# Loading the first image in pieces ahead of the weights, the second ahead of the zero fills, and moving the second image's statistics

## The chip, the cores and the metric

The kernel runs on one core of a Trainium2 chip. The metric is the device time of one execution in microseconds (us); less is better. One core has TensorE (PE in the profile, its weight loads PEld), VectorE (DVE), ScalarE (ACT), GpSimd (POOL) and SyncE (SP), each with its own queue of instructions that it runs in order, and 16 DMA engines.

## The reference, cut to what matters

Four images of 56 x 56 positions and 128 channels pass through four layers. Each layer normalizes its input by groups of four channels over the whole image, applies a block and adds the result to its input.

```python
def _gn(v, G=32, eps=1e-5):
    B_, H_, W_, C_ = v.shape
    g = v.reshape(B_, H_, W_, G, C_ // G)
    m = jnp.mean(g, axis=(1, 2, 4), keepdims=True)
    s = jnp.var(g, axis=(1, 2, 4), keepdims=True)
    return ((g - m) / jnp.sqrt(s + eps)).reshape(v.shape)

x = x + L0(_gn(x))   # window attention 7x7, full attention over 3136 positions, MLP
x = x + L1(_gn(x))   # projection, 3x3 depthwise convolution, selective scan in four directions, gate
x = x + L2(_gn(x))   # deformable 3x3 convolution (gathers at computed places)
x = x + L3(_gn(x))   # as L0, with weights of its own
```

What matters here: the group norm of a layer needs the sums over a whole image before anything of that layer can begin, and the images are independent of each other.

## The kernel before, in words

An image lies in fast memory as 128 channels x 3136 positions of float32 (1568 KB). Two such buffers exist, `xs[0]` and `xs[1]`; image b uses `xs[b % 2]`. The work on an image is cut into seven pieces of 448 positions (`NCK` pieces of `CH`).

*Start.* `__init__` loads the packs of weights: "C" (constants) and "L1" on SyncE's queue, "L0" and "L3" on ScalarE's, by `load` (L115 in the profile). It sets small constants. Then `run` issues the load of image 0 as one transfer (L1521), calls `swin_prepare` for L0 and L3 (one small matmul each, L198, and an addition, L199, which need that layer's weights), `mamba_prepare` (an exponential on ScalarE, L759, and two small operations on VectorE, L760 and L762, on weights of L1) and `deform_prepare`. The latter fills four tables in main memory with zeros, one for each image, from one small tile of zeros: for each table a transfer of 3364 KB (L1297) and one of 1 KB (L1300), on SyncE's queue. Behind them `run` issues the load of image 1 (L1526).

*Statistics.* `stats(b, c)` (L123) is one `bn_stats` on VectorE over piece c of image b. `group_norm` puts the seven together (L143), takes group means with a matmul (`gn_pm`, L145), the variance with another (`gn_pv`, L152), and the root on ScalarE (L154).

*The loop over images.* For each image `run` emits the seven statistics and then layer L0's attention, its MLP together with L1's convolution, L1's scan and L1's output; L2 of an image is woven beside the next image's L0 and L1, and L3 follows. For images that come later the statistics follow the loading of each piece at the end of L3 of the image that had the buffer before (`finish`, L1504 and L1506).

*The order.* Most stages are written under a manual schedule, which keeps the order of the code. Outside of these, and between stages, a scheduler places instructions in each engine's queue. VectorE's statistics of image 1 are emitted at the head of the loop's second turn; nothing before them writes that buffer, and the scheduler has put them far ahead of their place in the code, into the window stage of image 0.

*The window stage* (`windows`, inside `attention`) works through bands of windows: tokens (L243), projections (L251), scores (L276), their maxima and subtraction (L282, L283), exponentials (L286), normalization (L290, L291, and L294 on GpSimd), transposes (L300), and the full attention's inputs for the piece that is ready (L423 to L431) and first row maxima (L368, L373). After it comes the main attention loop, whose first matmuls are L540 and L549.

*L1's output stage* (`mamba_out`) runs a pipeline over seven pieces: mean, subtraction (L1226) and squares (L1228), gate (L1240), root (L135, L136), scaling (L1252, L1254), gating (L1258), the output matmul (L1264), and `store`, which adds the result to x (L1267) and takes the piece's statistics for L2 (L123).

Of the kernel before, what the change touches and what calls it, by code (L numbers as in the profile page):

```python
# [10 lines left out]
F32 = mybir.dt.float32  # L11
# [8 lines left out]
P = 128  # L20
HW = 56
L = HW * HW
CH = 448
NCK = L // CH
# [54 lines left out]
class _Net:  # L79
    def __init__(self, ctx, tc, x, packs, out):  # L80
        self.tc, self.nc, self.x_in, self.out, self.packs = tc, tc.nc, x, out, packs
        self.B = x.shape[0]
        nc = self.nc
        wp = ctx.enter_context(tc.tile_pool(name="weights", bufs=1))
        self.keep = wp
        self.w = {}
        for i, layer in enumerate(("C", "L0", "L1", "L3")):
            self.load(layer, wp, nc.sync if i % 2 == 0 else nc.scalar)
        c = self.w["C"]
        self.ident, self.gmat = c["ident"], c["gmat"]  # L90
        self.ones = {1: c["ones1"], 2: c["ones2"]}
        self.center = {1: (c["center1"],), 2: (c["center2"], c["others2"])}
        self.sel = wp.tile([P, KB], F32R, tag="sel", name="sel")
        nc.vector.memset(self.sel.bitcast(F32), 0.0)
        for h in range(NH):
            nc.vector.memset(self.sel[h * DK : h * DK + 2, :].bitcast(F32), 1.0)
        self.ident2 = wp.tile([64 + NX, NX], F32R, tag="ident2", name="ident2")
        nc.vector.memset(self.ident2.bitcast(F32), 0.0)
        for k in (0, 64):
            nc.vector.tensor_copy(self.ident2[k : k + NX, :], self.ident[:NX, :NX])  # L100
        self.all1 = wp.tile([P, P], F32, tag="all1", name="all1")
        nc.vector.memset(self.all1, 1.0)
        self.one32 = self.all1[:, :DK]
        self.eps = wp.tile([P, 1], F32, tag="eps", name="eps")
        nc.vector.memset(self.eps, 1e-5)
        self.any = wp.tile([P, 1], F32, tag="any", name="any")
        self.xs = [wp.tile([P, L], F32, tag=f"x{i}", name=f"x{i}") for i in range(2)]
        self.sts = [wp.tile([P, NCK, 6], F32, tag=f"gn_st{i}", name=f"gn_st{i}") for i in range(2)]
        self.dpool = ctx.enter_context(tc.tile_pool(name="tables", bufs=1, space=DRAM))

# [1096 lines left out]
    def mamba_out(self, b, ya, gn):  # L1207


        nc, tc, w, x = self.nc, self.tc, self.w["L1"], self.x_of(b)  # L1210
        with tc.tile_pool(name="mo", bufs=2) as sb, tc.tile_pool(name="mo_ps", bufs=8, space=PSUM) as ps, tc.manual_schedule():
            bank = lambda name: ps.tile([P, 512], F32, tag="mm", name=name)
            part = lambda c: slice(c * CH, (c + 1) * CH)
            m = {}

            def mean(c):
                pm = m["pm", c] = bank("pm")
                for j in range(2):
                    nc.tensor.matmul(pm[:, :CH], lhsT=self.center[2][1], rhs=ya[:, j, part(c)], start=(j == 0), stop=(j == 1))

            def less(c):
                pm = m.pop(("pm", c))
                xc = m["xc", c] = sb.tile([P, 2, CH], F32, tag="xc", name="xc", bufs=4)
                sq = m["sq", c] = sb.tile([P, 2, CH], F32, tag="sq", name="sq")
                for j in range(2):
                    nc.vector.tensor_add(xc[:, j, :], pm[:, :CH], ya[:, j, part(c)])  # L1226
                for j in range(2):
                    nc.scalar.activation(sq[:, j, :], xc[:, j, :], AF.Square)  # L1228

            def tokens(c):  # L1230
                m["xg", c] = sb.tile([P, CH], F32, tag="xg", name="xg2")
                self.gn_apply(m["xg", c], x[:, part(c)], gn)

            def gate(c):
                xg = m.pop(("xg", c))
                z = m["z", c] = sb.tile([P, 2, CH], F32, tag="z", name="z", bufs=3)
                for j in range(2):
                    pz = bank("pz")
                    nc.tensor.matmul(pz[:, :CH], lhsT=w["w_in"][:, (2 + j) * P : (3 + j) * P], rhs=xg, start=True, stop=True)
                    nc.scalar.activation(z[:, j, :], pz[:, :CH], AF.Silu)  # L1240

            def spread(c):
                sq, pv = m.pop(("sq", c)), bank("ln_pv")
                for j in range(2):
                    nc.tensor.matmul(pv[:, :CH], lhsT=self.all1, rhs=sq[:, j, :], start=(j == 0), stop=(j == 1))
                rs = m["rs", c] = sb.tile([P, CH], F32, tag="rs", name="rs")
                self.table_of_both()
                self.one_over_root(rs, pv[:, :CH], 0.5 / P)

            def scale(c):  # L1250
                xc, rs = m["xc", c], m.pop(("rs", c))
                nc.vector.tensor_mul(xc, xc, rs[:, None, :].to_broadcast([P, 2, CH]))  # L1252
                for j in range(2):
                    nc.scalar.activation(xc[:, j, :], xc[:, j, :], AF.Identity, bias=w["ln_b"][:, j : j + 1], scale=w["ln_w"][:, j : j + 1])  # L1254

            def gated(c):
                xc = m["xc", c]
                nc.vector.tensor_mul(xc, xc, m.pop(("z", c)))  # L1258

            def out(c):  # L1260
                xc = m.pop(("xc", c))
                po = m["po", c] = bank("pmo")
                for j in range(2):
                    nc.tensor.matmul(po[:, :CH], lhsT=w["w_out"][:, j * P : (j + 1) * P], rhs=xc[:, j, :], start=(j == 0), stop=(j == 1))  # L1264

            def store(c):
                nc.vector.tensor_add(x[:, part(c)], x[:, part(c)], m.pop(("po", c))[:, :CH])  # L1267
                self.stats(b, c)

            def do(f, c):  # L1270
                if 0 <= c < NCK:
                    f(c)

            tokens(0)
            for c in range(-1, NCK + 1):
                do(mean, c + 1)
                do(gated, c - 1)
                do(less, c + 1)
                do(scale, c)
                do(gate, c + 1)  # L1280
                do(out, c - 1)
                do(tokens, c + 2)
                do(spread, c + 1)
                do(store, c - 1)
# [233 lines left out]
            self.weave(self.mlp("L3", b, x1, oT, True, side is None), side)  # L1518

    def run(self):  # L1520
        self.nc.sync.dma_start(self.xs[0], self.x_in[0])  # L1521
        self.swin_prepare("L0")
        self.swin_prepare("L3")
        self.mamba_prepare()
        self.deform_prepare()
        self.nc.sync.dma_start(self.xs[1], self.x_in[1])  # L1526
        for b in range(self.B):
            for c in range(NCK):
                self.stats(b, c)
            with ExitStack() as mb:  # L1530
                s1, made = ExitStack(), {}
                made["at"] = self.swin_attention("L0", b, s1)
                self.weave(self.first_half(b, s1, mb, made, b == 0), self.deform(b - 1) if b > 0 else None)
                self.mamba(b, made["pool"], made)
            if b > 0:
                self.last_layer(b - 1, self.deform(b) if b == self.B - 1 else None)
        self.last_layer(self.B - 1)
# [91 lines left out]
```

## Time and profile before

| | us |
|---|---|
| median of 3 runs | 12171.69 |
| lowest and highest | 12166.93, 12178.63 |
| the profiled execution | 12171.84 |
| its span in the profile | 12169.8 |

| engine | busy us | share of the span |
|---|---|---|
| PE | 10926.0 | 90% |
| DVE | 9400.2 | 77% |
| POOL | 9398.7 | 77% |
| ACT | 7551.3 | 62% |

The granted clock of TensorE had a mean of 0.956 of full speed. Lines of the timeline read: start in us, duration in us, engine, line of the kernel, operation, output and inputs, count, and in brackets the idle time before it and what ended that. "SPq" is SyncE's queue issuing a transfer. Lines of the waits read: who waited, for whom, then us in total, times, and the longest.

### The profile page before, as it was taken

The numbers are of one execution on the slowest core, as the hardware profiler recorded it, in microseconds if no ns is written. First come the engines' busy times: TensorE is split into PE (matmuls) and PEld (weight loads), VectorE is DVE, ScalarE is ACT, GpSimd is POOL, SyncE is SP. The second block draws the span as 40 slices with busy tenths as digits, with TensorE's granted clock in tenths as the row PEclk, the third lists the DMA queues.
The fourth block names the chain that finished last, engine by engine and source line by source line (L and its number), as shares of the span: only waits on it lengthen the run. The fifth ranks groups of instructions, "written<-read, shape, count | busy, mean of one in ns | idle before, by whom it ended". The sixth has DMA issues, their size and how long they took to land.

```text
span 12169.8 us, 219808 instructions
## 1 busy us (share of the span) xinstructions
PE 10926.0 (90%) x86844; PEld 7148.8 (59%) x86844; DVE 9400.2 (77%) x12051; ACT 7551.3 (62%) x19326; POOL 9398.7 (77%) x5876
## 2 busy tenths in 40 slices
PE   5998998998799989999879988999988998997799
PEld 3546886553588845454368875545446886553454
DVE  4758997775999967477699986747679998775674
ACT  3667776564577656656467775665646776564366
POOL 1976997596799939669679985957957997596497
PEclk8999999998899999999989999999988999998899
DMA  1000000004300000000420000000051000004200
GB/s 65 2 1 17 5 5 2 1 1 124 97 6 5 3 1 1 12 1 2 142 79 5 5 3 1 2 12 1 1 169 53 6 5 2 1 1 137 73 2 6
DMA packets 145431, 321.09 MB, mean 26 GB/s; under 512 B 17885, under 2 KB 86673, under 8 KB 144145
## 3 DMA queue, kind: packets, MB, share of 16 engines
q0 software_dynamic: 70848, 231.27, 6.5%
q1 hardware_dynamic: 73264, 74.17, 1.9%
q8 instruction: 686, 11.24, 0.4%
q14 instruction: 345, 2.82, 0.1%
q10 hardware_dynamic: 288, 1.59, 0.0%
HBM read 259.05 MB, written 47.90 MB: 25 GB/s over the span
## 4 chain that ended last, share of the span: by engine, by line
PE 59%; DVE 16%; POOL 11%; ACT 8%; issue 4%; SPq 1%; DMA 1%; DVEq 0%; POOLq 0%; ACTq 0%
PE pm L368 15%; PE po L576 10%; DVE hs L1123 10%; POOL hs L1132 8%; PE pst L549 7%; PE pst L540 3%; PE pd L565 2%; PE yt L1141 2%; PE pyb L1162 2%; PE pvt L1455 2%; PE dbu L1105 2%; PE pdo L1463 1%; DVE dgb L1009 1%; DVE mx L373 1%; PE pc L819 1%
## 5 line engine op out<-in xcount | busy, mean ns | idle before, releaser
L373 DVE TENSOR_REDUCE mx<-pm 128x1 f32<-128x512 f32 (+7 forms) x6424 | 3377.7, 560 | 996.7 <-PE pm L368 920.0
L560 POOL TENSOR_TENSOR es<-es,e 128x896 f32<-128x896 f32 x1824 | 3764.5, 2090 | 78.5 <-ACT e L550 30.7
L1123 DVE TENSOR_TENSOR_SCAN hs<-da,dbu 128x928 f32<-128x928 f32 x1792 | 3617.5, 2068 | 33.7 <-ACT dbu L1116 17.4
L550 ACT ACTIVATE e<-pst 128x448 f32<-128x448 f32 (+1 forms) x5600 | 2592.6, 549 | 1534.7 <-PE pst L549 1123.4
L1132 POOL TENSOR_TENSOR hs<-hs,cb 128x896 f32<-128x896 f32 x1792 | 3434.5, 1948 | 18.9 <-ACT carry L1127 16.7
L368 PE MATMUL pm<-ks,qs 32*128 32x448 f32 (+5 forms) x12848 | 2966.3, 529 | 103.6 <-DVE mx L373 90.3
L549 PE MATMUL pst<-qs,ks 32*128 32x448 f32 x11200 | 2326.0, 540 | 0.0
L368 PEld LDWEIGHTS pm<-ks,qs 32*128 32x128 f32 x12848 | 1282.7, 187 | 1209.7 <-DVE mx L373 712.3
L1141 PE MATMUL yt<-w_C,hs 128*116 128x128 f32 x14336 | 1877.7, 274 | 15.0 <-POOL hs L1132 13.3
L540 PE MATMUL pst<-nm,sel 32*128 32x448 f32 x5600 | 1667.7, 527 | 6.9 <-DVE nm L394 6.9
L1141 PEld LDWEIGHTS yt<-w_C,hs 128*116 128x116 f32 x14336 | 1569.4, 135 | 39.3 <-POOL hs L1132 29.3
L1105 PE MATMUL dbu<-dgb,ut 112*128 112x224 f32 x7168 | 1249.4, 297 | 202.1 <-DVE hs L1123 199.7
L576 PE MATMUL po<-e,va 128*32 128x448 f32 (+1 forms) x11200 | 1360.1, 554 | 0.0
L1330 POOL DMA_INDIRECT g<-tab,idx x900 | 871.0, 968 | 507.2 <-issue 207.0
L549 PEld LDWEIGHTS pst<-qs,ks 32*128 32x128 f32 x11200 | 1255.8, 187 | 1.5
L1060 ACT ACTIVATE da<-dl,A 128x112 f32<-128x112 f32 x3584 | 1193.3, 382 | 0.1
L1105 PEld LDWEIGHTS dbu<-dgb,ut 112*128 112x128 f32 x7168 | 947.8, 192 | 322.2 <-DVE hs L1123 309.8
L540 PEld LDWEIGHTS pst<-nm,sel 32*128 32x128 f32 x5600 | 711.7, 185 | 165.9 <-issue 147.7
L294 POOL TENSOR_TENSOR pz<-s,m 64x784 f32<-64x784 f32 x128 | 191.8, 1499 | 776.9 <-DVE m L291 772.4
L1127 ACT COPY carry<-hs 128x32 f32<-128x32 f32 x1792 | 396.0, 221 | 550.6 <-DVE hs L1123 529.5
L576 PEld LDWEIGHTS po<-e,va 128*32 128x32 f32 (+1 forms) x11200 | 222.9, 108 | 826.0 <-issue 766.2
L1077 PE MATMUL pt<-w_C,dh 128*112 128x128 f32 x3584 | 552.5, 278 | 154.1 <-DVE dgb L1009 148.0
(227 smaller groups left out, 14350.8 us busy)
## 6 DMA issues: line engine op xcount, KB each, us to landing
g<-tab,idx POOLq DMA_INDIRECT x900, 3.6
tab<-zero SPq DMA_DIRECT2D x4, 3364.0 KB
dl_d<-dl SPq DMA_DIRECT2D x28, 448.0 KB
dl<-dl_d SPq DMA_DIRECT2D x56, 224.0 KB
tab<-gt SPq DMA_DIRECT2D x16, 448.0 KB
out_dram<-x SPq DMA_DIRECT2D x28, 224.0 KB
tab<-gt SPq DMA_DIRECT2D x16, 336.0 KB
w_L<-in_L_dram SPq DMA_DIRECT2D x4, 973.0 KB
```

The costliest lines, as they stand in the source:

```text
L368: nc.tensor.matmul(pm[:, at : at + m], lhsT=qs[head(h), q : q + P], rhs=ks[head(h), keys], start=True, stop=True)
L373: nc.vector.tensor_reduce(mx[:, i, h, n : n + 1], p, AX.X, ALU.max)
L540: nc.tensor.matmul(pst[g, h][:, :CH], lhsT=self.sel[head(h), :], rhs=nm[head(h), part(g // NKB)], start=True, stop=False)
L549: nc.tensor.matmul(t[:, :CH], lhsT=ks[head(h), k * KB : (k + 1) * KB], rhs=qs[head(h), part(qc)], start=False, stop=True)
L550: nc.scalar.activation(es[g, p][:nk, j, :], t[:nk, :CH], AF.Exp, scale=SCALE)
L560: nc.gpsimd.tensor_tensor(s, es[g - 1, p][:nk] if k == 1 else s, es[g, p][:nk], ALU.add)
L576: nc.tensor.matmul(m["po"][head(h), :CH], lhsT=va[:nk, k, head(h)], rhs=src(h)[:nk], start=(k == 0), stop=(k == NKB - 1))
L1060: nc.scalar.activation(m["da"][:, :, n, 2:], dl(), AF.Exp, scale=A[:, j, n : n + 1])
L1105: nc.tensor.matmul(pu[:, 8 * h : 8 * h + 8, 2 + tb * TB : 2 + (tb + 1) * TB], lhsT=made[g]["ut", 2 * r + tb][:, d, :], rhs=made["r", g // ...
L1123: nc.vector.tensor_tensor_scan(flat(pairs[u // 2][:, d % 2]), flat(made[g]["da"][:, r]), flat(banks.pop(u)), 0.0, ALU.mult, ALU.add)
L1132: nc.gpsimd.tensor_tensor(hs, hs, made["r", g // 2]["cb"][:, :, r * HW : (r + 1) * HW], ALU.mult)
L1141: nc.tensor.matmul(sums[q][:YR, e * P : (e + 1) * P], lhsT=hs[:, n, :], rhs=self.ident, start=(n == 0), stop=(n == NST // 2 - 1), is_trans ...
```

## The change

Image 0 is loaded in seven pieces of 448 positions (224 KB each) at the very front of SyncE's queue; L0 and C are loaded on ScalarE's queue, L1 and L3 on SyncE's behind the pieces. Image 0's statistics are emitted before the preparations. Image 1 is loaded, still as one transfer, before the zero fills. Image 1's statistics are no longer emitted at the head of its turn but in `store` of L1's output stage of image 0, one piece after each of image 0's pieces.

```diff
         self.w = {}
-        for i, layer in enumerate(("C", "L0", "L1", "L3")):
-            self.load(layer, wp, nc.sync if i % 2 == 0 else nc.scalar)
+        self.xs = [wp.tile([P, L], F32, tag=f"x{i}", name=f"x{i}") for i in range(2)]
+        for c in range(NCK):
+            cols = slice(c * CH, (c + 1) * CH)
+            nc.sync.dma_start(self.xs[0][:, cols], x[0][:, cols])
+        for layer, queue in (("L0", nc.scalar), ("C", nc.scalar), ("L1", nc.sync), ("L3", nc.sync)):
+            self.load(layer, wp, queue)
...
-        self.xs = [wp.tile([P, L], F32, tag=f"x{i}", name=f"x{i}") for i in range(2)]
...
             def store(c):
                 nc.vector.tensor_add(x[:, part(c)], x[:, part(c)], m.pop(("po", c))[:, :CH])
                 self.stats(b, c)
+                if b == 0:
+                    self.stats(1, c)
...
     def run(self):
-        self.nc.sync.dma_start(self.xs[0], self.x_in[0])
+        for c in range(NCK):
+            self.stats(0, c)
         self.swin_prepare("L0")
         self.swin_prepare("L3")
         self.mamba_prepare()
+        self.nc.sync.dma_start(self.xs[1], self.x_in[1])
         self.deform_prepare()
-        self.nc.sync.dma_start(self.xs[1], self.x_in[1])
         for b in range(self.B):
-            for c in range(NCK):
-                self.stats(b, c)
+            if b > 1:
+                for c in range(NCK):
+                    self.stats(b, c)
```

In each engine's list of instructions the change shows as follows. SyncE's and ScalarE's loads stand in the new order. TensorE's and GpSimd's lists are the same as before. VectorE's list has image 0's statistics and their aggregation ahead of L1's and L3's preparations, has lost the seven statistics in the window stage of image 0, and has seven more in its L1 output stage, the last of them ahead of image 1's aggregation. ScalarE's list has one more table load at the start: the table of the root is loaded first, then that of the exponential for `A` (L759), then that of the root again before the root itself.

## The prediction

> **What bounds the kernel now.** The profiled execution took 12171.84 us for a span of 12169.8 us; the median of the runs is 12171.69 us, so a saving in the span can be taken off either. Over the whole span TensorE leads (PE 59% of the chain that ended last), and the change touches none of its work. I therefore read the waits of the first 260 us, the stretch that the diff rearranges.
>
> ```profile
> POOL pz L294 <- DVE m L291: 180.5, 8, 106.5
> ACT oTi L418 <- DVE ln_sq L415: 97.9, 5, 94.9
> DVE gn_st L123 <- DMA x<-in_x_dram: 95.9, 2, 92.8
> PE pm L368 <- DVE mx L373: 90.3, 1, 90.3
> ```
>
> Columns: total, times, longest. Every engine has one wait of 90 to 106 us, and all of them lead to VectorE (DVE), which itself waits 92.8 us for a load of x. The timeline of DVE shows which one; the last two lines are the same steps for the second image.
>
> ```profile
> 71.07 0.56 DVE L282 TENSOR_REDUCE m<-pss 128x8 f32<-128x392 f32 x1
> ...
> 73.25 1.16 DVE L373 TENSOR_REDUCE mx<-pm 128x1 f32<-128x448 f32 x2
> 167.22 0.63 DVE L123 BATCH_NORM_STATS2 gn_st<-x 128x6 f32<-128x448 f32 x1 [92.82 <-DMA x<-in_x_dram]
> ...
> 182.92 0.56 DVE L282 TENSOR_REDUCE m<-pss 128x8 f32<-128x392 f32 x1
> ...
> 2142.84 0.56 DVE L282 TENSOR_REDUCE m<-pss 128x8 f32<-128x392 f32 x1
> ...
> 2159.37 0.56 DVE L282 TENSOR_REDUCE m<-pss 128x8 f32<-128x392 f32 x1
> ```
>
> Image 1's statistics (L123) stand in DVE's order in the middle of image 0's window stage, between two row maxima (L373) that need nothing of them. Their data is not there, and everything behind them stops. Why it is not there is seen in SyncE's queue:
>
> ```profile
> 3.35 40.39 SPq L1300 DMA_DIRECT2D tab<-zero  x1
> ...
> 50.86 33.94 SPq L1300 DMA_DIRECT2D tab<-zero  x1
> ...
> 87.36 32.33 SPq L1300 DMA_DIRECT2D tab<-zero  x1
> ...
> 122.75 34.41 SPq L1300 DMA_DIRECT2D tab<-zero  x1
> 157.21 0.91 SPq L1526 DMA_DIRECT2D x<-in_x_dram  x1
> ```
>
> The load of image 1 (L1526) is issued at 157.21, behind four zero fills of 3364 KB; ten us later it is there. In the windows, 100 to 125 us has no work on any engine, 97 GB/s and a TensorE clock of 0.50. So this is a pure stall, not a slow stage.
>
> **The stall (removed).** The two rows L282 are 111.85 us apart in image 0 and 16.53 us in image 1, which runs the same steps without it: 95.3 us. That includes the seven statistics (3.9 us) and the cold restart. The other end: from the group norm's first matmul to the first score matmul (L540) image 0 takes 286.49 - 17.98 = 268.5 us and image 1 2264.54 - 2087.76 = 176.8 us, 91.7 us less. Image 1 pays 1.9 us in that stretch that image 0 does not (a table load, memsets on GpSimd), so like for like it is 93.6 us. The remaining 1.7 us is a dip of the granted clock in image 1 (0.89 from 2226 to 2236) that image 0 lacked. I take 94.5 us, the middle.
>
> The fills (four of some 35 us, from about 14 us on) now run beside image 0's window stage until about 165 us. I cost this at nothing: 53.30 to 71.07 us, from L282 to L282, was 17.77 us with fills running, and the same step of image 1 (2125.04 to 2142.84) 17.80 us without. SyncE has nothing after them until the store at 916.46 us, so nobody is queued behind them. If that cover failed by a tenth over 95 us it would cost 9.5 us.
>
> **The start (shortened).** Before:
>
> ```profile
> 9.85 0.56 PE L198 MATMUL prep<-w_L 128*128 128x1 f32 x2 [3.13 <-DMA w_L<-in_L_dram]
> ...
> 13.72 3.78 DVE L123 BATCH_NORM_STATS2 gn_st<-x 128x6 f32<-128x448 f32 x7 [3.11 <-DMA x<-in_x_dram]
> ...
> 17.98 0.56 PE L145 MATMUL gn_pm<-gn_mv,w_C 128*128 128x1 f32 x2 [7.57 <-issue]
> ```
>
> Image 0 came last (13.6 us), then seven statistics (3.78) and the aggregation (0.34) stood on the path. Now the seven statistics run as the pieces land, and what lands last is L3's weights. TensorE is in order, so the group norm's first matmul (L145) now stands behind the preparation matmul of L3 (L198). DVE has the additions of that preparation and L1's two small operations (0.85 and 0.61) in front of `gn_mean`; these wait for weights that land earlier or together.
>
> The bytes ahead of the last landing are the same: image 0, C, L0, L1 and L3, 4.19 MB. The windows gave 420 GB/s from 4 to 12 us, and the last of it was usable at 13.6. In the changed program's instruction list the seventh piece waits for L0's landing (6.1 us before) and L3 for the second piece. About 2 us lie between an issue and its first bytes (issue at 0.74, flow from about 2.8), so the seventh piece starts at some 8.3 us; the six earlier pieces, L0 and C are 2.57 MB and occupy the engines until 2.8 + 6.1 = 8.9. So no gap, and L3 lands at 13.6 again; L145 runs some 0.35 us later, at 14.0 instead of 17.98: **4.0 us gained**. Ends: 5.4 if L3 is usable when the bytes are through (12.2), and a loss of 4.1 if the pieces don't overlap (a rival below).
>
> ScalarE gains one table load (1.28 us): the exponential of A now stands between the early load of the root's table and its use. It carries no wait and follows A, whose L1 weights land some 1.9 us (0.79 MB at 420 GB/s) before L3's, while the root's input is made 1.6 us after L3. So it is hidden; uncovered it costs 1.28. The Trainium skill ("ScalarE: Activation LUTs", What ACT_TABLE_LOAD costs) adds about 1.4 us of drain to each switch; the trace shows none (load at 9.28 for 1.28, next activation at 10.57), so its figure would only make an uncovered load 2.7.
>
> **The output stage of image 0 (seven statistics added).** DVE runs 7 x 0.63 = 4.4 us more there. A steady turn takes 7.42 us and is closed by ScalarE (two table loads, gate, root, squares, scaling), with DVE waiting for it:
>
> ```profile
> 2049.95 1.09 DVE L1252 TENSOR_TENSOR xc<-xc,rs 128x896 f32<-128x896 f32 x1 [2.46 <-ACT rs L136]
> ...
> 2057.37 1.09 DVE L1252 TENSOR_TENSOR xc<-xc,rs 128x896 f32<-128x896 f32 x1 [2.46 <-ACT rs L136]
> ```
>
> The 2.46 us take a statistic of 0.63. What is queued behind it, the gating L1258 and the mean's subtraction L1226, ends at 55.5 instead of 54.9, and the squares are due at 57.24. Only the last two turns are bare: the gating (2082.19) starts 0.3 later, and two statistics of 0.57 now precede the aggregation at 2087.27, which preceded its one. Of these 1.5 us, 0.46 is DVE's idle time before the windows of image 1: **1.0 us lost**; ends 0 and 4.4.
>
> **Sum.** -94.5 - 4.0 + 1.0 = -97.5: 12171.84 - 97.5 = **12074 us**.
>
> **Rivals.**
> The small prices are all paid: the statistics cost 4.4 and the table load 1.3. -94.5 - 4.0 + 4.4 + 1.3 = -92.8, **12079 us**. For it: both stand in in-order queues. Against it: the slack above. 12%.
>
> The pieces land one after the other. A 224 KB piece of a later image took from its issue at 5052.67 to its statistic at 5055.20, 2.53 us. Seven in a row end at 0.74 + 17.7 = 18.4, L1 and L3 (1.39 MB) 3.3 us later, L145 at 22.1: 4.1 us lost instead of 4.0 gained, **12082 us**. Against it: the three loads issued at 0.74, 1.18 and 1.65 moved at 420 GB/s together. 8%. The Trainium skill ("DMA: Bandwidth & Descriptors", Bandwidth) speaks for this rival: batch transfers to 1 MiB and more; its fit of 2.0 us plus bytes over 436 GB/s gives the same 2.53 us a piece, but it is for one DMA, and the trace shows several in flight.
>
> The stall stays, because something else needs image 1 or the fills early: **12172 us**. Against it: the load goes out before the fills, and no instruction of the first 2000 us reads image 1 any more. 3%.
>
> Slower: the idle 90 us buy a high clock later, and without them the throttle takes more. TensorE's 59% of the chain are 7180 us; the granted mean is 0.956, and from 0.943 down the loss exceeds 97 us. At 0.940 it is 7180 x (0.956/0.940 - 1) = 122, **12196 us**. Against it: 350 to 750 us, after the stall, and 2328 to 2728, with no stall before it, both had 1.00. 2%.
>
> **How the numbers follow.** The forecast's own case has 75%. The bounds of the costs give 95.3 + 5.4 = 100.7 saved (12071) to 12082; the spread of the runs before, -5 and +7 around their median, and clock dips of 1.7 us widen this to 12064 to 12088. A measurement of this kernel can tell about 0.2% (24 us) from no change: 0.95 faster (75 + 12 + 8), 0.03 the same, 0.02 slower.
>
> **What would show it.** Right: no wait of DVE on x over 10 us before 260 us; rows L282 17 us apart; the first L145 near 14 us; turns of 7.4 us in image 0's output stage; the first L540 near 188 us (286.49 - 94.5 - 4.0). Wrong: L145 past 18 us, window turns well over 18 us while the fills run, a mean clock under 0.95.

## The result, and the profile after

| | before | after |
|---|---|---|
| median of 4 runs, us | 12169.31 | 12069.99 |
| lowest and highest | 12146.61, 12178.63 | 12056.44, 12079.11 |
| profiled execution | 12171.84 | 12079.11 |
| its span | 12169.8 | 12077.3 |
| its mean granted clock | 0.956 | 0.959 |

The changed kernel takes 0.992 of the time of before, with a 95% interval of 0.9903 to 0.9937. The median is 4 us below the forecast of 12074, and the profiled execution 5 us above it; the interval by itself leaves anything from 77 to 118 us of gain. All later experiments ran on other chips, on which the kernel before had medians of 12233 to 12239 us; totals are therefore compared as ratios to the runs of before on the same chip, and places inside the first 2000 us by their times. In the changed kernel's files the lines stand a little lower: L123 is L126, L145 is L148, L282 is L285, L540 is L543, L1252 is L1255, L1526 is L1531.

The waits of the first 200 us of the changed kernel (who waited for whom, total, times, longest):

```profile
POOL pz L297 <- DVE m L294: 84.6, 8, 15.6
...
ACT oTi L421 <- DVE ln_sq L418: 5.6, 6, 2.5
...
DVE gn_st L126 <- DMA x<-in_x_dram: 4.4, 3, 3.2
```

The three groups that had one wait of 92.8 to 106.5 us each have none over 15.6 left. VectorE's longest wait for x is 3.2 us, and it is for the first piece of image 0. VectorE's timeline shows the place where the stall was:

```profile
67.63 0.56 DVE L285 TENSOR_REDUCE m<-pss 128x8 f32<-128x392 f32 x1
...
69.80 2.22 DVE L376 TENSOR_REDUCE mx<-pm 128x1 f32<-128x448 f32 x4
...
84.17 0.56 DVE L285 TENSOR_REDUCE m<-pss 128x8 f32<-128x392 f32 x1
```

From L285 to L285 it is 16.54 us, where it was 111.85; image 1 of before had 16.53. The four row maxima (L376) stand in one piece now. SyncE's queue shows why nothing waits, and that the fills run beside this stage:

```profile
0.74 5.53 SPq L90 DMA_DIRECT2D x<-in_x_dram  x7
...
8.10 0.33 SPq L1531 DMA_DIRECT2D x<-in_x_dram  x1
...
9.64 37.83 SPq L1305 DMA_DIRECT2D tab<-zero  x1
...
130.68 34.19 SPq L1305 DMA_DIRECT2D tab<-zero  x1
```

Image 1's load goes out at 8.10 instead of 157.21, and the last fill's issue ends at 164.9. The long issues carry the line of the 1 KB transfer behind each large fill (L1305): the queue stands there while 3364 KB go out ahead of it (some 35 us at 95 GB/s). The 16.54 us step between 67.63 and 84.17 lies in the middle of them.

The start, on TensorE and then on VectorE:

```profile
14.28 0.56 PE L201 MATMUL prep<-w_L 128*128 128x1 f32 x2 [7.72 <-DMA w_L<-in_L_dram]
15.09 0.59 PE L148 MATMUL gn_pm<-gn_mv,w_C 128*128 128x1 f32 x2 [0.25 <-DVE boe_L L202]
```

```profile
11.43 0.35 DVE L146 BATCH_NORM_AGGREGATE gn_mv<-gn_st 128x2 f32<-128x42 f32 x1
...
14.87 0.16 DVE L202 TENSOR_TENSOR boe_L<-prep,w_L 128x1 f32<-128x1 f32 x1 [2.14 <-PE prep L201]
```

The statistics of image 0 are put together at 11.43 us, but the group norm's matmul runs at 15.09: it stands in TensorE's order behind the preparation of L3, whose weights arrive last. That is 2.9 us earlier than before (17.98).

The output stage of image 0, on VectorE (two steady turns, and the end):

```profile
1955.03 1.09 DVE L1255 TENSOR_TENSOR xc<-xc,rs 128x896 f32<-128x896 f32 x1 [2.13 <-ACT rs L139]
...
1957.11 1.15 DVE L126 BATCH_NORM_STATS2 gn_st<-x 128x6 f32<-128x448 f32 x2
...
1962.45 1.09 DVE L1255 TENSOR_TENSOR xc<-xc,rs 128x896 f32<-128x896 f32 x1 [2.13 <-ACT rs L139]
...
1992.61 1.15 DVE L126 BATCH_NORM_STATS2 gn_st<-x 128x6 f32<-128x448 f32 x2
1993.80 0.34 DVE L146 BATCH_NORM_AGGREGATE gn_mv<-gn_st 128x2 f32<-128x42 f32 x1
...
1998.43 2.84 DVE L246 TENSOR_SCALAR xw<-x,gn_mean,gn_rstd 128x343 f32<-128x343 f32 x1 [0.46 <-DVE gn_rstd L158]
```

A turn is still 7.42 us (1962.45 - 1955.03); the second statistic has come out of the wait for ScalarE, which is 2.13 instead of 2.46. At the end two statistics stand before the aggregation where none stood before (image 0's last one ran behind it, at 2087.53), and there is again an idle time of 0.46 us before the windows of image 1. The first of the windows' operations (1998.43) took 2.84 us, beside a memset of GpSimd; before, it took 0.59:

```profile
1999.25 1.80 POOL L249 MEMSET pz<- 128x2048 f32 x1
2001.82 1.64 PE L254 MATMUL pq<-xw,w_L 128*128 128x392 f32 x2 [5.68 <-DVE xw L246]
```

Image 1's first projection (L254, L251 before) starts 7.53 us after its gn_pm (1994.29); before, it was 5.34 us. The account below comes back to this.

### The profile page after: what moved, and what is told of

Read it like the earlier page. It is cut to its first block, busy times and chain, and to the rows that moved or that the text cites. A ratio compares the mean times of both kernels' runs of the same rounds, so it can differ in the third digit from the quotient of the medians.

```text
span 12077.3 us, 219818 instructions
## 1 busy us (share of the span) xinstructions
PE 10924.2 (90%) x86844; PEld 7150.1 (59%) x86844; DVE 9398.6 (78%) x12051; ACT 7556.4 (63%) x19327; POOL 9397.2 (78%) x5876
## 4 chain that ended last, share of the span: by engine, by line
PE 59%; DVE 16%; POOL 11%; ACT 9%; issue 4%; DMA 1%; DVEq 0%; POOLq 0%; ACTq 0%; SPq 0%
PE pm L371 15%; PE po L579 10%; DVE hs L1126 9%; POOL hs L1135 9%; PE pst L552 7%; PE pst L543 3%; PE pd L568 2%; PE yt L1144 2%; PE pyb L1165 2%; PE dbu L1108 2%; PE pvt L1460 2%; DVE dgb L1012 1%; PE pdo L1468 1%; DVE mx L376 1%; ACT da L1063 1%
## 5 line engine op out<-in xcount | busy, mean ns | idle before, releaser
L376 DVE TENSOR_REDUCE mx<-pm 128x1 f32<-128x512 f32 (+7 forms) x6424 | 3377.5, 560 | 999.9 <-PE pm L371 924.1
L543 PE MATMUL pst<-nm,sel 32*128 32x448 f32 x5600 | 1666.4, 527 | 6.9 <-DVE nm L397 6.9
L543 PEld LDWEIGHTS pst<-nm,sel 32*128 32x128 f32 x5600 | 710.5, 185 | 164.3 <-issue 145.5
```

The costliest lines, as they stand in the source:

```text
L376: nc.vector.tensor_reduce(mx[:, i, h, n : n + 1], p, AX.X, ALU.max)
L543: nc.tensor.matmul(pst[g, h][:, :CH], lhsT=self.sel[head(h), :], rhs=nm[head(h), part(g // NKB)], start=True, stop=False)
```

## The experiments

Theory: the whole gain is the stall, and the stall needs two things at once, statistics of image 1 early in VectorE's order and its load behind the zero fills. Taking away either removes all of it; the loading in pieces gives a few us at most, and the fills cost nothing beside the window stage. Rival: the gain comes from the new start, or is spread over the parts, or fills that run under the window stage cost something that only the whole change makes good.

**Image 1's load alone ahead of the fills**, nothing else changed from before.

```diff
         self.mamba_prepare()
-        self.deform_prepare()
         self.nc.sync.dma_start(self.xs[1], self.x_in[1])
+        self.deform_prepare()
```

> Of the change only one part: image 1 is loaded before the zero fills; its statistics stay where the scheduler puts them (early in image 0's first stages), image 0 is one transfer behind C and L1, as before. Theory (the stall is the fills ahead of the load): the load lands some 4 us after image 0's, near 17.5 us, and the stall goes, less the seven statistics (3.9 us) and up to 2 us in the group norm of image 0, behind which one of them now waits: 88 to 93 us less than before, about 12080. Rival (the place of the statistics is the cause, the load order is beside the point): no change, 12170.

Measured: 12144.13 us, ratio 0.9917 (0.99 to 0.9934), as much as the whole change. The timeline of VectorE in this kernel, with the statistics still early in its order:

```profile
18.40 0.62 DVE L123 BATCH_NORM_STATS2 gn_st<-x 128x6 f32<-128x448 f32 x1
19.53 0.61 DVE L123 BATCH_NORM_STATS2 gn_st<-x 128x6 f32<-128x448 f32 x1
21.61 2.73 DVE L123 BATCH_NORM_STATS2 gn_st<-x 128x6 f32<-128x448 f32 x5
```

The data is there, so the seven statistics of image 1 run at 18 to 24 us between other work, without a wait. The scheduler has placed them even earlier than before (where the wait for them began at 74.4 us), so the edit of one line moves both the load and the statistics; what it takes away is the late data, not the early place. The first L540 starts at 188.3, a microsecond before that of the changed kernel, although gn_pm (17.28) has gained little; the granted clock was higher in its window stage (0.94 against 0.89 from 15 to 45 us, 1.00 against 0.94 from 135 to 165). One moved line is enough for all that the total can show.

**Image 1's statistics alone moved to the output stage**; the load stays behind the fills.

```diff
             def store(c):
...
                 self.stats(b, c)
+                if b == 0:
+                    self.stats(1, c)
...
         for b in range(self.B):
-            for c in range(NCK):
-                self.stats(b, c)
+            if b != 1:
+                for c in range(NCK):
+                    self.stats(b, c)
```

> Of the change only another part: image 1's statistics move to the output stage of image 0; image 1 is still loaded behind the four fills, image 0 is still one transfer. Theory (nothing else of the first 2000 us needs image 1): the stall goes completely although the load still lands at 167 us; 94.5 - 1.0 = 93.5 us less, about 12078. Rival (the fills themselves hold something up, the load's place in the queue matters): a wait of tens of us stays before 170 us, and the time lies between 12100 and 12170.

Measured: 12158.18 us, ratio 0.9926 (0.9909 to 0.9942). SyncE's queue, then the waits of the first 200 us:

```profile
157.63 2.23 SPq L1528 DMA_DIRECT2D x<-in_x_dram  x1
```

```profile
POOL pz L294 <- DVE m L291: 84.8, 8, 15.6
...
DVE gn_st L123 <- DMA x<-in_x_dram: 3.0, 1, 3.0
```

The load is as late as in the kernel before (157.63 against 157.21), and nothing waits for it: the first L540 is at 192.5. So the late load was no cost by itself, nor were the early statistics. The two removals in the change do the same thing twice.

**The new start alone**: pieces, order of the weights and early statistics of image 0 as in the change, image 1 as before.

```diff
-        for i, layer in enumerate(("C", "L0", "L1", "L3")):
-            self.load(layer, wp, nc.sync if i % 2 == 0 else nc.scalar)
+        for c in range(NCK):
+            cols = slice(c * CH, (c + 1) * CH)
+            nc.sync.dma_start(self.xs[0][:, cols], x[0][:, cols])
+        for layer, queue in (("L0", nc.scalar), ("C", nc.scalar), ("L1", nc.sync), ("L3", nc.sync)):
+            self.load(layer, wp, queue)
...
-        self.nc.sync.dma_start(self.xs[0], self.x_in[0])
+        for c in range(NCK):
+            self.stats(0, c)
...
         for b in range(self.B):
-            for c in range(NCK):
-                self.stats(b, c)
+            if b > 0:
+                for c in range(NCK):
+                    self.stats(b, c)
```

> Of the change only the start: image 0 in seven pieces ahead, the new order of the weights, statistics of image 0 before the preparations; image 1 behind the fills and its statistics at the head of its turn, as before. Theory (a stall that ends at a time set by the DMA queue swallows what is gained ahead of it): the first gn_pm comes 2.9 us earlier as in the changed kernel, but DVE then waits until image 1 lands, some 4 us later than before because the first fill is issued at 9 us and not at 2.5; 0 to 4 us slower than before, 12170 to 12176. Rival (the parts add up): 2.9 us faster, 12169.

Measured: 12243.52 us, ratio 1.0001 (0.9991 to 1.0011). SyncE's queue and VectorE's timeline:

```profile
164.94 3.30 SPq L1530 DMA_DIRECT2D x<-in_x_dram  x1
```

```profile
177.84 0.63 DVE L126 BATCH_NORM_STATS2 gn_st<-x 128x6 f32<-128x448 f32 x1 [104.89 <-DMA x<-in_x_dram]
```

The first gn_pm comes at 14.89, 3.1 us earlier than in the profile of before, and the first L543 at 295.8, 9.3 us later. The stall ends when the load lands, whatever the work ahead of it does. The load goes out 7.7 us later: 5.5 because the first fill is issued behind the pieces (8.03 instead of 2.48), the rest within the fills. Its data is used 10.6 us later (177.84 instead of 167.22), where I had expected some 4. Faster work ahead of a wait only lengthens the wait (104.89 instead of 92.82). The 9 us are within what the interval of the ratio allows (plus or minus 12 us); the total neither confirms nor denies them.

**The change with image 0 as one transfer** at the head of the queue.

```diff
-        for c in range(NCK):
-            cols = slice(c * CH, (c + 1) * CH)
-            nc.sync.dma_start(self.xs[0][:, cols], x[0][:, cols])
+        nc.sync.dma_start(self.xs[0], x[0])
```

> The changed kernel with image 0 as one transfer at the head of SyncE's queue in place of seven pieces; all else as changed. Theory (L3's weights end the start, not image 0): image 0 lands at 8 to 9 us, its statistics are done by 13, L3 lands at 13.6 to 14.2, and the first gn_pm comes at 14.3 to 15.1 us as with the pieces (15.09); no change of the total, 12070. Rival (the pieces are what shortens the start): the seven statistics stand on the path again, gn_pm at 17 to 18 us. Rival of the prediction (pieces don't overlap): gn_pm clearly earlier than 15.09, under 13.5.

Measured: 12142.39 us, ratio 0.9919 (0.9902 to 0.9935). TensorE's timeline, then VectorE's:

```profile
13.51 0.56 PE L199 MATMUL prep<-w_L 128*128 128x1 f32 x2 [3.60 <-DMA w_L<-in_L_dram]
16.43 0.58 PE L146 MATMUL gn_pm<-gn_mv,w_C 128*128 128x1 f32 x2 [2.36 <-DVE boe_L L200]
```

```profile
11.78 0.37 DVE L102 CAST ident<-w_C 40x40 fp32r<-40x40 f32 x2 [1.68 <-DMA w_C<-in_C_dram]
12.17 3.79 DVE L124 BATCH_NORM_STATS2 gn_st<-x 128x6 f32<-128x448 f32 x7
...
16.02 0.34 DVE L144 BATCH_NORM_AGGREGATE gn_mv<-gn_st 128x2 f32<-128x42 f32 x1
```

A miss: I had reckoned that L3's weights would close the start here too. They were used 0.8 us earlier than with pieces (13.51 against 14.28), but the seven statistics had not run meanwhile. VectorE's order has the cast of the constants ahead of them, and C arrived at 11.78. Then the statistics took 3.79 us in a row. So the pieces are worth 1.3 us at gn_pm (16.43 against 15.09): they take the statistics off the path and cost 0.8 us in the loads. With the cast behind the statistics one transfer might do as well; this was not tried. The total cannot show any of it.

**Each zero fill twice, in the kernel before.** The kernel does the fills twice and is otherwise the one before.

```diff
             for t in self.tables:
-                nc.sync.dma_start(
-                    t[: TR * TR].rearrange("(a b) c -> a b c", a=116), z[:, None, :].to_broadcast([116, TR * TR // 116, 2 * P])
-                )
+                for _ in range(2):
+                    nc.sync.dma_start(
+                        t[: TR * TR].rearrange("(a b) c -> a b c", a=116), z[:, None, :].to_broadcast([116, TR * TR // 116, 2 * P])
+                    )
```

> The kernel before with each of the four zero fills issued twice (the same zeros again). Theory (the length of the stall is the length of the fills ahead of image 1's load): four more fills of about 36 us put the load at 300 us instead of 157, the wait of DVE grows from 92.8 to 235 to 240 us, and the total by 143 to 147 us, about 12315. Rival (the wait has another cause that ends near 167 us): no change.

Measured: 12387.01 us, ratio 1.0122 (1.0102 to 1.0142). SyncE's queue, VectorE's timeline, and two windows of the stall (us, busy time of each engine, clock, DMA share, GB/s):

```profile
43.84 81.46 SPq L1298 DMA_DIRECT2D tab<-zero  x3
...
195.80 119.76 SPq L1298 DMA_DIRECT2D tab<-zero  x3
...
350.57 8.71 SPq L1527 DMA_DIRECT2D x<-in_x_dram  x1
```

```profile
369.33 0.63 DVE L123 BATCH_NORM_STATS2 gn_st<-x 128x6 f32<-128x448 f32 x1 [263.30 <-DMA x<-in_x_dram]
```

```profile
125.00:160.00 35.00, 0.00 (x0) 0.00 (x0) 0.00 (x0) 0.00 (x0) 0.00 (x0) 0.50 0.27 93
196.00:235.00 39.00, 0.00 (x0) 0.00 (x0) 0.00 (x0) 0.00 (x0) 0.00 (x0) 0.50 0.21 61
```

The direction is the theory's: longer fills move the load and the stall with it. The load goes out 193 us later, where I had expected 143. Part of the fills ran at 61 GB/s instead of 93: the three issues at 195.80 took 119.76 us, the same three at 43.84 took 81.46. What slowed them is open. It wasn't the window stage, since no engine worked in either window, and doubling alone does not bring it, as the next run shows. The wait, on the other hand, grew by 170.5 us only (263.30 against 92.82), because the scheduler had placed the statistics later in VectorE's order: the wait begins at 106.0 us instead of 74.4. The first L540 came at 454.9, 168.4 us later than in the profile of before; the interval of the ratio is 125 to 174 us.

**Each zero fill twice, in the changed kernel**, the same edit.

> The changed kernel with each of the four zero fills issued twice. Theory (with the load ahead of them and the statistics away, nobody waits for the fills, and they cost nothing beside the work): fills until about 310 us, no wait for them, the first L543 at 189 us as without, 12070. Rival (fills beside running engines slow them): stages up to 310 us longer by some per cent, 3 to 10 us.

Measured: 12141.55 us, ratio 0.9921 (0.9902 to 0.9941). SyncE's queue, then the waits:

```profile
280.67 33.20 SPq L1306 DMA_DIRECT2D tab<-zero  x1
```

```profile
POOL pz L297 <- DVE m L294: 85.2, 8, 15.6
```

The fills now last until 314 us, through the whole window stage and into the main attention loop, and the first L543 starts at 189.6 against 189.4. The same edit costs 1.2% where a load stands behind the fills, and nothing that can be measured where none does. All eight fills ran at the old pace here (82.05 and 82.12 us for three issues). This pair shows the mechanism most plainly: it isn't the fills' traffic that costs time, but a load behind them in the queue for which an early instruction waits.

**L3's weights late**: in the changed kernel their load stands behind image 1's, and the preparation is emitted at the head of L3 of image 0.

```diff
-        for layer, queue in (("L0", nc.scalar), ("C", nc.scalar), ("L1", nc.sync), ("L3", nc.sync)):
+        for layer, queue in (("L0", nc.scalar), ("C", nc.scalar), ("L1", nc.sync)):
...
     def last_layer(self, b, side=None):
+        if b == 0:
+            self.swin_prepare("L3")
...
         self.swin_prepare("L0")
-        self.swin_prepare("L3")
         self.mamba_prepare()
         self.nc.sync.dma_start(self.xs[1], self.x_in[1])
+        self.load("L3", self.keep, self.nc.sync)
         self.deform_prepare()
```

> The changed kernel with L3's weights loaded behind image 1 and its preparation moved to the head of the first L3 turn. Theory (the start ends with L3's landing because the group norm's matmul stands behind L3's preparation): gn_pm follows the aggregation at 11.5 to 12 us instead of 15.09, 3 us earlier; in the instruction list the root also comes before A's exponential, so the additional table load is gone. First L543 near 186, total 3 us less, 12067, too little to be told from the changed kernel by the time alone. Rival (image 0's last piece or C ends the start): gn_pm stays after 14 us.

Measured: 12145.01 us, ratio 0.9925 (0.9909 to 0.9942). TensorE's timeline:

```profile
11.77 0.56 PE L148 MATMUL gn_pm<-gn_mv,w_C 128*128 128x1 f32 x2 [5.36 <-DVE gn_mv L146]
```

gn_pm now waits for the aggregation alone and comes at 11.77, 3.3 us earlier than in the changed kernel; the first L543 comes at 185.3, 4.1 us earlier. So what closed the changed kernel's start was L3, as the prediction had it.

**Both corrections**: L3 late, and image 1's statistics two to a turn in the first four turns, so that none stands in the last.

```diff
                 if b == 0:
-                    self.stats(1, c)
+                    for k in range(2 * c, min(2 * c + 2, NCK)):
+                        self.stats(1, k)
```

> As the one with L3 late, and image 1's seven statistics two at a time in the first four turns of the output stage, so that none stands in the last three. Theory: each turn has 2.46 us of slack for 1.15 more, turns stay at 7.42 us, and the aggregation of image 1 comes 0.9 to 1.2 us earlier after the last output matmul than in the changed kernel: 12066. Rival (two statistics a turn are too many): turns of 7.6 us or more.

Measured: 12141.26 us, ratio 0.9917 (0.9901 to 0.9934). VectorE's timeline:

```profile
1955.02 1.09 DVE L1255 TENSOR_TENSOR xc<-xc,rs 128x896 f32<-128x896 f32 x1 [1.60 <-ACT rs L139]
...
1992.34 0.34 DVE L146 BATCH_NORM_AGGREGATE gn_mv<-gn_st 128x2 f32<-128x42 f32 x1
```

The wait for ScalarE takes two more statistics per turn as easily as one (1.60 left of 2.46), and the turn stays at 7.4 us. From the last mean's matmul to image 1's gn_pm it is 19.7 us, 1.5 less than in the changed kernel (21.2) and about what it was before (19.8). From gn_pm to the first projection it is 4.9 us instead of 7.5, so that at this place the version gains 4.1 us in all.

This version and the changed kernel then ran five times each on one chip.

> The changed kernel itself, in the same call as the version with a late load of L3 and two statistics in each of four turns, so that the two can be compared directly. Its own trace gave the first L543 at 189.4 and the second gn_pm at 1994.3; both are expected here within 1 us. Ratio to the kernel before: 0.992.

> The version with a late load of L3 and two statistics in each of four turns once more. If the 2.8 us at the first L543 and the 1.5 us at the end of image 0 stay in the total, its median is 4 us below that of the changed kernel in this call (0.04%); if the scatter of the granted clock (22 us between the runs of the changed kernel) decides, the two medians lie within 10 us either way and their order tells nothing.

Measured: 12136.87 us (12131.98 to 12147.29), ratio 0.9922 (0.9908 to 0.9935), for the changed kernel and 12140.23 us (12135.07 to 12143.47), ratio 0.9922 (0.9909 to 0.9936), for the version with both corrections. TensorE's timelines, the changed kernel first:

```profile
15.10 0.59 PE L148 MATMUL gn_pm<-gn_mv,w_C 128*128 128x1 f32 x2 [0.25 <-DVE boe_L L202]
...
1996.71 0.56 PE L148 MATMUL gn_pm<-gn_mv,w_C 128*128 128x1 f32 x2 [2.37 <-DVE gn_mv L146]
```

```profile
12.03 0.56 PE L148 MATMUL gn_pm<-gn_mv,w_C 128*128 128x1 f32 x2 [5.33 <-DVE gn_mv L146]
...
1987.13 0.35 PE L148 MATMUL gn_pm<-gn_mv,w_C 128*128 128x1 f32 x2 [1.06 <-DVE gn_mv L146]
```

The gains are in place again: 2.9 us at the first L543 (188.47 to 185.56), 1.5 between the last L1255 and image 1's gn_pm (1987.13 to 1996.71 is 9.58; 1979.00 to 1987.13 is 8.13), and 2.6 from there to the first projection (7.52 and 4.88). At image 1's gn_pm the corrected version led by 9.6 us in the two profiled executions, and its median was 3 us behind. The five runs of the changed kernel alone lie 15 us apart, so a lead of some 7 us can't be seen in the totals; where it goes in the other 10,000 us is not shown. Of the versions tried, none is shown to beat the changed kernel. One miss on the way: I expected the second gn_pm within 1 us of 1994.3, and it came at 1996.71.

## Why the prediction was right, step by step

*The stall*, 94.5 us. The rows L285 give 111.85 - 16.54 = 95.3, and the stretch from gn_pm to the first score matmul 268.5 - (189.38 - 15.09) = 94.2. The forecast of 94.5 lies between the two. That the stall went away entirely, and was not replaced by another, is shown by the waits, and its two conditions by the first two experiments. The prediction had treated the load's move and the statistics' move as one step; each alone is sufficient, which it did not say.

*The fills*, nothing. Shown in the changed kernel (16.54 us a step with fills, 16.53 without) and by doubling them. The bound of 9.5 us for a cover that fails was not needed.

*The start*, 4.0 us; measured 2.9 (17.98 to 15.09). This term was mis-sized in both of its numbers. L3 was used at 14.28, not 13.6: from 4 to 12 us the loads moved 403 GB/s, where I had taken over the 420 of the old order (430 in the same window of before). The experiment with one transfer has L3 at 13.51, and the new start alone, with pieces and on the same chip, at 14.08, so it is the pieces that cost 0.6 to 0.8 us. And L145 came 0.81 us behind L3's preparation, not 0.35. The trace names the cause, a wait of 0.25 us for VectorE's addition of that preparation (L202): I had put only TensorE's order between the two, not the way to VectorE and back.

*The rival of pieces one after the other* fell. Its seventh piece would have been in at 18.4; all seven statistics were done by 11.43. The pieces overlap: against one transfer the whole batch cost 0.8 us, the rival had over 8. The Trainium skill's fit for one transfer ("DMA: Bandwidth & Descriptors", Anatomy of one DMA — SWDGE (gpsimd) path), measured on transfers that GpSimd issues, does not add up over the seven here.

*The additional table load*, hidden. ScalarE's exponential for A ran at 12.29, the load at 12.54 for 1.28, and the root's input came at 16.99, after 3.17 us of idle time. So the load had 3.2 us of slack here, and no drain beside it appears in the trace.

*The output stage*, 1.0 us; measured 1.4 up to image 1's gn_pm (19.8 us from the last mean's matmul before, 21.2 after), and 2.2 more up to the first projection. This term was mis-sized. The turn absorbed its statistic as predicted. At the end I subtracted 0.46 us of VectorE's idle time before the windows as slack, but the idle time was there again (0.46 before and after), and behind it something came that the prediction had not priced. This is the first operation of the windows before, and in the version with both corrections:

```profile
2091.89 0.59 DVE L243 TENSOR_SCALAR xw<-x,gn_mean,gn_rstd 128x343 f32<-128x343 f32 x1 [0.46 <-POOL pz L246]
...
2093.10 1.65 PE L251 MATMUL pq<-xw,w_L 128*128 128x392 f32 x2 [3.50 <-DVE xw L243]
```

```profile
1996.61 0.48 DVE L246 TENSOR_SCALAR xw<-x,gn_mean,gn_rstd 128x343 f32<-128x343 f32 x1
...
1997.71 1.64 PE L254 MATMUL pq<-xw,w_L 128*128 128x392 f32 x2 [3.04 <-DVE xw L246]
```

In the changed kernel the same operation took 2.84 us. It started at 1998.43, beside GpSimd's memsets of kb and pz, which stood from 1997.90 to 2001.05, and ended at 2001.27, 0.22 us after them. GpSimd's memsets begin when the last output matmul ends and know nothing of the statistics. All six traces with two statistics ahead of the aggregation show this: the operation takes 2.84 to 3.40 us and ends 0.22 us after the memset, and the first projection comes 7.5 us after gn_pm. In the five other traces of the experiments and in the one of before, it takes 0.48 to 0.89 us, and the projection comes after 4.9 us (5.3 before).

So a delay of 1.3 us on VectorE (TensorE's wait for the aggregation is 2.37 instead of 1.06) pushed this operation beside work of another engine, and there it was longer. That the memset holds it was not tried by moving the memset, and what ends the 0.46 us is open: before, the profile names the memset, after, VectorE's own reciprocal, and in the version with both corrections there is no such wait. Together the term is 3.6 us at the first projection, inside the prediction's end of 4.4. Part of it seems to stay: from the last mean's matmul to image 1's first score matmul the six traces take 196 to 200 us, the five 194 to 195 (before, with its dip of the clock, 196.6).

*The sum.* Measured by place: 2.9 + 94.2 - 1.4 = 95.7 us, against 97.5. At image 1's gn_pm the trace has 93.5 (2087.76 to 1994.29), at its first projection 91.3 (2093.10 to 2001.82). On the way there is a dip of the granted clock at the end of image 0's scan, seen in the rows of TensorE, before and after:

```profile
2020.10 3.68 PE L1162 MATMUL pyb<-w_C,ys 116*128 116x56 f32 x32
```

```profile
1922.16 6.92 PE L1165 MATMUL pyb<-w_C,ys 116*128 116x56 f32 x32
```

With it the way from the last scan to the first mean took 13.7 us instead of 10.0. That makes 95.7 - 3.7 = 92.0; the 1.5 us between this and 93.5 I have not placed. The spans differ by 92.5 us and the medians by 99.3, on either side of the forecast. The start and the output stage both came out less good than forecast; that the median nevertheless lies within 4 us of the forecast is in part luck, since single runs of the changed kernel lie 23 us apart. The range also has a slip: by its own working its upper end is 12082 + 7 + 1.7, some 12091, not 12088.

*The slower rival*, a throttle that takes more because the idle 90 us are gone, fell: the mean clock of the four runs was 0.959 to 0.962, not below 0.943. The stall itself was the stretch with a granted clock of 0.50; doubling the fills, with a longer stall, gave 0.949. An estimate from these figures: taking 94.5 us at 0.50 out of a mean of 0.956 over 12169.8 us leaves 0.960, so the rest of the kernel was granted about what it had before.

## What to carry to other kernels

A stall of this kind has two halves, an instruction placed early in an in-order queue and its data placed late in another; look for both, and repair the cheaper one, since one is enough. Work saved ahead of a wait is worth nothing until the wait is gone. Before a small delay is set against an idle gap, look at what the delayed instructions will then run beside: here 1.3 us on VectorE moved an operation beside memsets of GpSimd, and it ended 2.2 us later still.

## What was not expected of the hardware

The granted clock drops to 0.50 for some 10 us behind pauses of TensorE of less than a microsecond, and whether it does differs between executions. Image 0's main attention shows it. Near its end TensorE waits twice in every trace; here in the second profiled execution of the changed kernel:

```profile
666.60 0.44 PE L394 MATMUL pmt<-w_C,n 128*128 128x128 f32 x2 [0.91 <-ACT n L387]
667.89 0.77 PE L543 MATMUL pst<-nm,sel 32*128 32x448 f32 x4 [0.86 <-DVE nm L397]
```

From 668 to 677 us the clock is 0.50 in this execution. In the first one the same two pauses (0.91 and 0.86, up to 668.87) were followed by a clock of 1.00. From its first L540 to its last the main attention takes 538 us in five of the twelve profiled executions and 543 in the seven that have the drop, so it costs 5 us; on one chip there were two of each. What decides it is not shown. The dip at the end of the scan, above, also stands behind pauses of TensorE (idle for 1.7 us of the three from 1918 to 1921, then 0.50). Over the whole kernel this fits the scatter, though nothing here shows it to be all of it: the runs of the changed kernel with 0.962 and with 0.959 are 22.7 us apart, and 0.003 of TensorE's 7180 us on the path is 21.5. Refinements below that size are to be read from the place, not from the total.

The chips differ by more than most edits do. On another chip the changed kernel's profiled execution took 57 us longer at nearly the same mean clock (0.958 against 0.959). The group of GpSimd's gathers in the profile differs by nearly as much, first chip and then second (busy, mean ns, idle before):

```profile
L1335 POOL DMA_INDIRECT g<-tab,idx x900 | 870.2, 967 | 505.9 <-issue 203.8
```

```profile
L1335 POOL DMA_INDIRECT g<-tab,idx x900 | 878.5, 976 | 549.3 <-issue 231.7
```

Busy and idle time together are 1376.1 and 1427.8, a difference of 51.7 us. Whether these lie on the path was not tried.

The zero fills use a part of the DMA engines: a share of 0.27 at 93 GB/s, where the loads of the start had all of them and over 400. The Trainium skill has a rule for how many engines share a transfer, the largest number up to 16 that divides the slowest dimension on both sides ("DMA: Bandwidth & Descriptors", Why a DMA increments its semaphore by 16 and not by 1). For 116 partitions that makes four, by estimate a share of 0.25; the trace agrees with its 0.27.
